# A graph network's planner for five engines gives way to an order written out step by step

## The chip, the cores and the metric

The kernel runs on one core of one Trainium2 chip. A core has five engines that each work through a queue of their own in order: TensorE (PE, matrix products into PSUM banks; PEld is its loading of weights), VectorE (DVE), ScalarE (ACT), GpSimd (POOL) and SyncE (SP), which here only issues DMAs. Engines wait for one another through semaphores. The metric is the device time of one execution in microseconds; smaller is better.

## The reference

Thirty-two graphs ("frames") of 512 nodes with 256 features pass through four attention layers, all with the same 512 x 512 adjacency. After each layer comes x = layernorm(x + layer(x)).

```python
# layer 0: 8 heads of 32, then a two-layer MLP
scores = q k^T / sqrt(32);  attn = softmax(where(adj > 0, scores, -1e9))
x1 = LN(x + attn v) * g1 + b1
y  = LN(x1 + relu(x1 w1 + bias1) w2 + bias2) * g2 + b2
# layer 1: e = leaky_relu(s1[n] + s2[m], 0.2), masked softmax, times h = x W
# layer 2: e = leaky_relu((x W1)(x W2)^T, 0.2), masked softmax, times x W3, relu
# layer 3: as layer 1 with 4 heads of 64, then elu
```

All of it is in float32.

## The kernel before

`fast_path` holds the frames' computation. It doesn't issue instructions as it goes; it describes each frame as steps (`Op`), with the engine, an assumed time in ns, the function that issues the instructions, and the buffers read and written. `Plan.__call__` finds from the buffers which step needs which. A frame has 74 steps on PE, 95 on DVE, and fewer than 130 on each other engine; 32 frames and the preparation of weights and mask make 2391 steps on PE, 3087 on DVE, 3911 on ACT, 884 on POOL and 245 on SP. `plan.place` then puts the steps in order in a model of the engines, `plan.emit` issues them in that order, and the engines' queues get exactly this order. About six frames are in flight at once.

What sets the order: `graph(0)` is placed alone first, which gives each step its place in tenths of a frame (`when`). `due` turns that into a due time: `PACE` 81.87 us per frame, plus a table of where each tenth should stand (`TENTHS`, with other tables for the first four and the last five frames). At each point `place` takes, among the steps that can start soonest, the one that is due first. `safe` refuses a step that could leave no buffer for an earlier frame. A step that needs a buffer gets the one of its kind that, in the model, came free first. Buffers are shared by all frames: 8 PSUM banks, 8 "p" (128 x 4 x 512, attention weights), 9 "t", 7 "y", 6 "x", 4 "e", 3 "v" and some small ones.

Steps of a frame that the prediction names, by the line that issues them:

- L1376 on SP loads x. L932 (`transposed`) transposes 128 x 128 blocks on PE; L1047 does so for the heads' outputs, L1015 for the softmax sums (`sums_back`).
- L749 (`product`) is every full-width product: projections, the MLP, layers 1 and 2. It can be issued as whole 128*128 products, or cut into four with 32 columns of weights each (128*32); `emit` chooses, with the assumed costs of a change of form in `CHANGE`.
- Layer 0, per group g of four heads and block m of 128 nodes: L1064 (`exps`) forms four heads' scores with 32 rows each (32*128) in four banks; ACT takes exp of them (L1068) into a p; DVE multiplies p by the mask (L1116); L1123 multiplies by v (128*32). For the softmax sums, the p's are added up by DMAs that POOL issues (L1002, `add_dma`), then halves are folded, then SP copies one half (L1142), and L1095 sums over the partitions. The last frame sums on PE alone.
- Layer 1: L749 makes v; `gates` sends one column through ACT, a transpose (L1212), a DMA to DRAM (L1216) and a DMA that broadcasts it to all partitions (L1222); DVE makes four blocks of p (L1241) and masks them (L1244); L749 multiplies p by v.
- Layer 2: L749 makes scores, ACT and DVE the masked exponentials, L749 the output.
- Layer 3: as layer 1, with four heads; DVE L1320 (four) and L1327 make a p, L1335 multiplies by q (128*32), L1311 sums.
- `normalise` (L973 to L983): statistics on DVE, the root on ACT, the scaling on ACT.

The array's forms matter to the text below: a matmul record of form 32*128 or 128*32 is one of four that run side by side. An f32 product shows as two records.

Of the kernel before, what the change touches and what calls it, by code (L numbers as in the profile page):

```python
# [9 lines left out]
FP = mybir.dt.float32  # L10
# [19 lines left out]
WAYS = 6  # L30
PACE = 81.87
STAY = 0.00
START = (0, 10.17, 59.24, 97.18, 85.64)
EARLY = 186.52

TENTHS = (0, 35.72, 65.32, 68.92, 152.58, 202.32, 246.27, 266.73, 356.34, 362.66, 490.49)
FIRST = (
    (0, 35.72, 65.32, 62.35, 138.44, 202.98, 246.27, 266.73, 356.34, 362.66, 490.49),
    (-28.44, 35.72, 73.98, 55.02, 197, 202.32, 246.27, 266.73, 356.34, 362.66, 490.49),
    (-31.13, 30.72, 65.32, 68.92, 152.58, 202.32, 246.27, 266.73, 356.34, 362.66, 490.49),  # L40
    (0, 35.77, 65.37, 68.97, 152.63, 202.32, 246.27, 266.73, 356.34, 362.66, 490.49),)
LAST = (
    (0, 35.72, 65.32, 68.92, 152.58, 202.32, 246.27, 266.73, 354.73, 363.36, 490.49),
    (0, 35.72, 65.32, 68.92, 152.58, 202.32, 246.27, 266.73, 356.34, 362.66, 490.49),
    (0, 35.72, 65.32, 68.92, 152.58, 202.26, 246.21, 266.73, 356.34, 412.91, 557.81),
    (-0.21, 35.51, 65.11, 68.71, 152.37, 202.11, 226.96, 232.14, 316.44, 341.17, 500.04),
    (-6.23, 29.49, 59.09, 8.93, 61.49, 76.67, 155.18, 191.54, 257.43, 316.36, 394.47),)
# [391 lines left out]
SIGNAL = 70  # L439
SWITCH = 100  # L440
CHANGE = {0: 196, 1: 213, 2: 126}


class Slot:
# [3 lines left out]
    def __init__(self, kind):  # L448
        self.kind, self.index, self.users, self.ends, self.graph = kind, None if kind else 0, 0, 0.0, None
        self.first = self.last = None  # L450


class Op:
    def __init__(self, engine, ns, run, graph, rank, port, lag, tiling, ways):
        self.engine, self.ns, self.run, self.graph, self.rank = engine, ns, run, graph, rank
        self.port, self.lag, self.tiling, self.ways = port, lag, tiling, ways
        self.then, self.missing, self.slots, self.ready = [], 0, [], 0.0


class Plan:  # L460
# [10 lines left out]
    def clear(self):  # L471
        self.ops, self.graph, self.rank, self.start = [], 0, 0, 0.0
        self.log = {}

    def begin(self, graph, start=0.0):


        self.graph, self.rank, self.start = graph, 0, start

    def __call__(self, engine, ns, run, reads=(), writes=(), port=False, lag=0, tiling=0, ways=None):  # L480
        op = Op(engine, ns, run, self.graph, self.rank, port, lag, tiling, ways or {tiling: 0})
        if not op.rank:
            op.ready = self.start
        self.rank += 1
        needs = {}
        for is_write, group in ((False, reads), (True, writes)):
            for item in group:
                slot, part = (item[0], item[1:]) if isinstance(item, tuple) else (item, None)
                if slot not in op.slots:
                    op.slots.append(slot)  # L490
                    slot.users += 1
                    if slot.first is None:
                        slot.first = op.rank
                    slot.last = op.rank
# [19 lines left out]
    def profile(self, graph):  # L514

        ops = [op for op in self.ops if op.graph == graph]
        live = {kind: [0] * len(ops) for kind in self.counts}
        for slot in {id(s): s for op in ops for s in op.slots if s.kind}.values():
            for r in range(slot.first, slot.last + 1):
                live[slot.kind][r] += 1  # L520
        return live

    def place(self, urgency, ways, stay=0.0, early=1e12,):
# [3 lines left out]
        held_by = {g: self.profile(g) for g in {op.graph for op in self.ops}}  # L527
        engines = {e: 0.0 for e in (PE, DVE, ACT, POOL, SP, DMA)}
        waiting = {e: [] for e in engines}
        free = {k: [(0.0, i) for i in range(n)] for k, n in self.counts.items()}  # L530
        todo, held = {}, {}
        for op in self.ops:
            todo.setdefault(op.graph, set()).add(op.rank)
            if not op.missing:
                waiting[op.engine].append(op)
        order, front, ended = sorted(todo), {g: 0 for g in todo}, {}
        port, port_by, end, tiling = 0.0, None, 0.0, 0
        self.trace = []

        def safe(op, kind, new):  # L540
            spare = len(free[kind]) - len(new)
            if spare < 0:
                return False
            have = spare
            for g in order:
                mine = held.get((g, kind), [])
                have += len(mine)
                if g == op.graph:
                    have += len(new)
                    mine = mine + new  # L550
                r, rows = front[g], held_by[g][kind]
                ahead = sorted(s.first for s in mine if s.first > r)
                for i, stop in enumerate(ahead + [len(rows)]):
                    if stop > r and max(rows[r:stop]) + len(ahead) - i > have:
                        return False
                    r = max(r, stop)
                if g == op.graph:
                    return True

        while todo:  # L560
            choice = None
            for e, ops in waiting.items():
                found = []
                for op in ops:
                    if order[0] + ways <= op.graph:
                        continue
                    due = urgency(op)
                    t = max(engines[e], op.ready, ended.get(op.graph - ways, 0.0))
                    if op.graph >= 0:
                        t = max(t, due - early)  # L570
                    if op.port and port_by is not e:
                        t = max(t, port)
                    if choice and t > choice[0]:
                        continue
                    wants = {}
                    for s in op.slots:
                        if s.index is None:
                            wants.setdefault(s.kind, []).append(s)
                    if all(safe(op, kind, new) for kind, new in wants.items()):
                        for kind, new in wants.items():  # L580
                            t = max(t, sorted(free[kind])[len(new) - 1][0])
                        if op.tiling != tiling and e is PE:
                            due += stay
                        found.append((t, due, op))
                if found:
                    best = min(found, key=lambda f: f[:2])
                    if choice is None or best[0] < choice[0]:
                        choice = best
            assert choice, "no instruction can be placed: too few buffers"
            t, _, op = choice  # L590
            if op.engine is PE and op.tiling != tiling:
                t, tiling = max(t, engines[PE] + SWITCH), op.tiling
            waiting[op.engine].remove(op)
            for s in op.slots:
                if s.index is None:
                    pick = min(free[s.kind])
                    free[s.kind].remove(pick)
                    s.index, s.graph = pick[1], op.graph
                    held.setdefault((op.graph, s.kind), []).append(s)
            engines[op.engine] = t + op.ns  # L600
            if op.port:
                port, port_by = t + op.ns, op.engine
            done = t + op.ns + op.lag + SIGNAL
            end = max(end, done)
            for s in op.slots:
                s.users -= 1
                s.ends = max(s.ends, done)
                if not s.users and s.kind:
                    free[s.kind].append((s.ends, s.index))
                    held[s.graph, s.kind].remove(s)  # L610
            for other in op.then:
                other.missing -= 1
                other.ready = max(other.ready, done if other.engine != op.engine or op.lag
                                  else t + op.ns)
                if not other.missing:
                    waiting[other.engine].append(other)
            left = todo[op.graph]
            left.remove(op.rank)
            while front[op.graph] not in left and left:
                front[op.graph] += 1  # L620
            ended[op.graph] = max(ended.get(op.graph, 0.0), t + op.ns + SIGNAL)
            if not left:
                del todo[op.graph]
                order.remove(op.graph)
# [842 lines left out]
```

## Time and profile before

| | us |
|---|---|
| median of 3 runs | 2871.28 (2866.46 to 2874.03) |
| the profiled execution | 2871.61 |
| its span, first to last instruction | 2869.7 |
| first product starts, last ends (from the span's start) | 7.7, 2852.4 |

Most of the span is periodic: TensorE repeats one order every 86 us, for example from 606.3 to 692.3 us. Busy shares in such a frame are about 100% for TensorE, 88% for VectorE, 68% for ScalarE, 31% for GpSimd; the DMA engines are busy 73% of the time.

| line, what | count | mean us of one |
|---|---|---|
| L1116 DVE mask of a p, layer 0 | 256 | 2.464 |
| L1327 DVE mask of a p, layer 3 | 128 | 2.423 |
| L1068 ACT exp of a bank | 1024 | 0.599 |
| L1002 POOL issue of an adding DMA | 372 | 0.873 |
| L990 POOL addition 128 x 512 | 192 of the form y<-y,x | 1.441 |

A profile's busy time is the sum of records. On ACT and DVE the next instruction starts before the record of the last one ends: the exps of L1068 follow each other at 0.477 us, the masks of L1116 at 2.20 us from start to start. On PE the records' ends are modelled, so times from start to start are used below.

The four parts of a frame's adding DMAs move 10 MB per frame, and they make up most of the DMA traffic: 325 of 425 MB.

### The profile page before, as it was taken

What the parts mean: (1) busy time and instruction counts of PE and PEld (TensorE: products, weight loads), DVE (VectorE), ACT (ScalarE), POOL (GpSimd) and SP (SyncE); (2) the same over time, 40 slices, a digit from 0 to 9 for tenths busy, and PEclk for the clock granted to TensorE, in tenths of its full rate; (3) what the DMA queues carried; (4) which work ended last, traced back from release to release, by engine and by line L of the source; (5) the groups of instructions that cost most, each with busy time, mean ns of one, the idle gap of its engine ahead of it and who ended that gap; (6) DMA issues with size and microseconds to landing.
All of it is one profiled execution on the core that took longest, in us unless ns stands there. A gap on an engine that the chain in (4) does not pass through costs nothing.

```text
span 2869.7 us, 49717 instructions
## 1 busy us (share of the span) xinstructions
PE 2802.0 (98%) x19058; PEld 1507.2 (53%) x19058; DVE 2436.6 (85%) x4076; ACT 1884.6 (66%) x4104; POOL 871.5 (30%) x962
## 2 busy tenths in 40 slices
PE   8889999999999999999999999999999999999996
PEld 3345455555555555555555555555555555554562
DVE  5467888988888988888888888998888998889877
ACT  4566667666676666676666676666676766677553
POOL 1223333323333223333323333323333323333312
PEclk9899999999999999999999999999999999999998
DMA  7855777777776777777777777777777777775115
GB/s 168 169 115 122 159 159 151 156 156 149 164 162 151 155 157 149 162 166 149 155 156 149 162 165 154 149 156 148 163 165 157 148 159 149 160 165 114 41 51 139
DMA packets 101188, 425.07 MB, mean 148 GB/s; under 512 B 10256, under 2 KB 46224, under 8 KB 59152
## 3 DMA queue, kind: packets, MB, share of 16 engines
q0 software_dynamic: 49600, 325.08, 57.6%
q1 hardware_dynamic: 51344, 96.75, 11.7%
q8 instruction: 152, 2.49, 0.3%
q14 instruction: 92, 0.75, 0.1%
HBM read 63.38 MB, written 17.10 MB: 28 GB/s over the span
## 4 chain that ended last, share of the span: by engine, by line
PE 87%; DVE 7%; DMA 2%; ACT 2%; issue 2%; POOL 0%; SPq 0%; DVEq 0%; ACTq 0%; POOLq 0%
PE bank L749 54%; PE bank L1064 8%; PE bank L1123 8%; PE bank L1335 7%; PE bank L932 4%; DVE p L1116 3%; PE bank L1047 2%; PE bank L1311 1%; PE bank L1095 1%; PE bank L1015 1%; DVE p L1320 1%; DMA x<-in_x_dram 1%; ACT p L1068 1%; DVE st L973 1%; DMA p<-p 0%
## 5 line engine op out<-in xcount | busy, mean ns | idle before, releaser
L1002 POOL DMA_DIRECT2D p<-p x372 | 323.3, 873 | 1766.4 <-DMA p<-p 587.7
L1116 DVE TENSOR_TENSOR p<-p,edge_t 128x2048 f32<-128x2048 f32 x256 | 628.5, 2464 | 61.4 <-ACT p L1068 61.2
L920 ACT ACTIVATE t<-bank 128x512 f32<-128x512 f32 x640 | 373.1, 595 | 393.6 <-PE bank L1123 129.9
L1068 ACT ACTIVATE p<-bank 128x512 f32<-128x512 f32 x1024 | 537.4, 599 | 81.9 <-PE bank L1064 81.5
L749 PE MATMUL bank<-v,p 128*128 128x257 f32 (+1 forms) x2912 | 468.0, 384 | 4.3 <-DVE p L1244 3.8
L749 PEld LDWEIGHTS bank<-v,p 128*128 128x128 f32 (+1 forms) x2912 | 367.7, 159 | 90.7 <-issue 26.6
L973 DVE BATCH_NORM_STATS2 st<-y 128x6 f32<-128x256 f32 x768 | 316.1, 412 | 36.2 <-POOL y L990 26.6
L1320 DVE TENSOR_SCALAR p<-p,e,e 128x512 f32<-128x512 f32 x512 | 333.1, 684 | 0.4 <-DMA p<-row 0.3
L990 POOL TENSOR_TENSOR y<-y,x 128x512 f32<-128x512 f32 x192 | 275.3, 1441 | 156.7 <-ACT y L1295 98.4
L1327 DVE TENSOR_TENSOR p<-p,edge_t 128x2048 f32<-128x2048 f32 x128 | 310.2, 2423 | 2.2
L1064 PE MATMUL bank<-t,t 32*128 32x512 f32 x2048 | 300.7, 646 | 0.0
L983 ACT ACTIVATE x<-y,rs,rs 128x256 f32<-128x256 f32 x512 | 277.7, 596 | 18.0 <-DVE rs L980 15.1
L1123 PE MATMUL bank<-p,v 128*32 128x512 f32 x2048 | 274.0, 607 | 15.2 <-DVE p L1116 11.4
L1335 PE MATMUL bank<-p,v 128*32 128x512 f32 x2048 | 241.5, 597 | 3.7 <-DVE p L1327 3.2
L749 PE MATMUL bank<-t,wqkv 128*32 128x512 f32 (+1 forms) x944 | 243.8, 596 | 0.9 <-ACT t L920 0.9
L920 ACT ACTIVATE v<-bank 128x264 f32<-128x264 f32 (+2 forms) x384 | 176.1, 459 | 80.0 <-PE bank L749 77.0
L749 PE MATMUL bank<-t,t 128*128 128x512 f32 (+1 forms) x656 | 225.2, 592 | 0.0
L1064 PEld LDWEIGHTS bank<-t,t 32*128 32x128 f32 x2048 | 84.1, 185 | 173.4 <-issue 86.4
L932 PE MATMUL bank<-ident,x 128*128 128x128 f32 x1024 | 149.6, 280 | 14.2 <-DMA x<-in_x_dram 10.3
L974 DVE BATCH_NORM_AGGREGATE mv<-st 128x2 f32<-128x6 f32 x768 | 139.9, 182 | 26.3
L932 PEld LDWEIGHTS bank<-ident,x 128*128 128x128 f32 x1024 | 118.2, 142 | 78.8 <-issue 37.7
L749 PEld LDWEIGHTS bank<-t,t 128*128 128x128 f32 (+1 forms) x656 | 94.3, 167 | 111.2 <-issue 107.2
(119 smaller groups left out, 3855.7 us busy)
## 6 DMA issues: line engine op xcount, KB each, us to landing
p<-p POOLq DMA_DIRECT2D x248, 1024.0 KB, 7.2
p<-p POOLq DMA_DIRECT2D x124, 512.0 KB, 5.8
p<-row SPq DMA_DIRECT2D x32, 1024.0 KB
x<-in_x_dram SPq DMA_DIRECT2D x32, 512.0 KB
out_dram<-x SPq DMA_DIRECT2D x32, 512.0 KB
p<-p SPq DMA_DIRECT2D x31, 512.0 KB
e<-row SPq DMA_DIRECT2D x32, 256.0 KB
t<-in_adj_dram SPq DMA_DIRECT2D x4, 256.0 KB
```

The lines of the kernel that those rows point to most:

```text
L749: nc.tensor.matmul(out[c:c + w, :], left[:, c:c + w], right, start=start, stop=stop)
L920: act(170 + n * 0.84, lambda: nc.scalar.activation(to(T(dst)), frm(T(src)), AF.Copy), [src], writes)
L932: nc.tensor.transpose(T(bank)[:, (2 * k + c) * P:(2 * k + c + 1) * P], T(src)[:, c0 + c, k * P:(k + 1) * P], ident)
L973: nc.vector.bn_stats(T(st)[:, c, :], T(y)[:, c, :])
L1002: nc.gpsimd.dma_start(a, b, accum_op=ALU.add)
L1064: nc.tensor.matmul(T(banks[j]), T(kT)[r, g, m * P:(m + 1) * P], T(qT)[r, g, :], start=True, stop=True)
L1068: act(600, lambda j=j: nc.scalar.activation(T(p)[:, j, :], T(banks[j]), AF.Exp, scale=1.0 / math.sqrt(D0)), [banks[j]], [(p, j)])
L1116: dve(2420, lambda p=p, m=m: nc.vector.tensor_tensor(T(p), T(p), T(edge_t)[:, m, :].unsqueeze(1).to_broadcast([P, J, N]), ALU.mult), [p, ( ...
L1123: nc.tensor.matmul(T(av)[j * D0:(j + 1) * D0, :], T(v)[:, m, h * D0:(h + 1) * D0], T(p)[:, j, :], start=(m == 0), stop=(m == NC - 1))
L1320: nc.vector.tensor_scalar(T(p)[:, 2 * m + i, :], T(G)[:, h, :], T(e1)[:, r:r + 1], T(e02)[:, r:r + 1], ALU.mult, ALU.max)
L1327: nc.vector.tensor_tensor(p4, p4, T(edge_t)[:, m0:m0 + 2, :].unsqueeze(2).to_broadcast([P, 2, 2, N]), ALU.mult)
L1335: nc.tensor.matmul(T(av)[w:w + 32, :], T(q)[:, m0 + m, 2 * H3 + k * P + w:2 * H3 + k * P + w + 32], T(p)[:, 2 * m + w // D3, :], start=(m0 ...
```

## The change

`place`, `profile`, the due times (`PACE`, `TENTHS`, `FIRST`, `LAST`, `START`, `EARLY`) and the placeholder steps (`skip`) are taken out. In their place stands ORDER: for each engine a string. A letter stands for a frame (A to Z, a to f; "." for the preparation) and means "the next step of this frame on this engine that hasn't been issued"; a number ahead of it skips so many of those. `follow` walks the five strings with a model of the engines, and hands each step that needs a buffer the one that came free first in that model. The model's times are new. `ways` chooses the form of `product` along the whole PE string.

```diff
+GRAPHS = ".ABCDEFGHIJKLMNOPQRSTUVWXYZabcdef"
+ORDER = {
+    "PE": (
+        "1A1.2.A1.1..3A.1A1AAA2.2.1..A2.AB..1AB2AAB2A1BA2AAAB1A2B1B2AAB2AAAB1CA1BC2BB2BCBB1B2B1CCB1CC2BC3B1DB"
...
+    "SP": (
+        "A1.3.2.11.2.8.1.3.1.5.B.9.5..6.D1.2.2.2.2.C1..FEABAACBBAADCCBBEAGDDCCFBHEEDDGCIFFEEHDJGGFFEIKHHGGFJL"
...
-SIGNAL = 70
-SWITCH = 100
-CHANGE = {0: 196, 1: 213, 2: 126}
+SIGNAL = 40
+SWITCH = 92
+ENTRY = {1: 121, 2: 34}
+TAIL = {PE: 160, DVE: 85, ACT: 120, POOL: 130, SP: 0, DMA: 0}
+IDLE, SPAN, SLOW = 1500, 2000, 1700
...
-    def place(self, urgency, ways, stay=0.0, early=1e12,):
...
+    def ways(self, order):
...
+        costs, steps = {0: 0.0, 1: 1e15, 2: 1e15}, []
+        for op in order:
+            came, new = {}, dict.fromkeys(costs, 1e15)
+            for way, extra in op.ways.items():
+                cost = {w: c + (SWITCH + op.enter(way) if w != way else 0) for w, c in costs.items()}
+                came[way] = min(cost, key=cost.get)
+                new[way] = cost[came[way]] + extra
+            costs = new
+            steps.append(came)
...
+    def follow(self, order):
...
+        for e, steps in order.items():
+            queues[e], at = [], 0
+            for step in steps:
+                if step.isdigit():
+                    at = 10 * at + int(step)
+                else:
+                    queues[e].append(left[e, GRAPHS.index(step) - 1].pop(at))
+                    at = 0
+        self.ways(queues[PE])
...
+            for s in op.slots:
+                if s.index is None:
+                    s.index = free[s.kind].pop(0)[1]
...
-        plan.place(urgency, WAYS, 1e3 * STAY, 1e3 * EARLY)
+        plan.follow(ORDER)
         plan.emit(tiling)
```

The assumed times of most steps change too; they are used by the model alone. Examples:

```diff
-        plan(PE, 970, run, [(kT, g), (qT, g)], banks, tiling=1)
+        plan(PE, 858, run, [(kT, g), (qT, g)], banks, tiling=1)
...
-            act(600, lambda j=j: nc.scalar.activation(
+            act(482, lambda j=j: nc.scalar.activation(
...
-                dve(2420, lambda p=p, m=m: nc.vector.tensor_tensor(
+                dve(2205, lambda p=p, m=m: nc.vector.tensor_tensor(
...
-        plan(POOL, 950, run, reads, [dst, started])
-        plan(DMA, 5600 if src else 2650, None, reads + [started], [dst], lag=2500)
+        plan(POOL, 850, run, reads, [dst, started], lag=300)
+        plan(DMA, 5000 if src else 2500, None, reads + [started], [dst], lag=1300 if src else 1900)
```

The instructions that a step issues are the same as before. The changed file also holds some text twice (the classes, the general path's layer functions and the head of `fast_path`); the later definitions replace the earlier ones.

## The prediction

> **What bounds the kernel now.** I read the page first, then the waits of TensorE in three stretches, the busy time by stretch, and the timeline of TensorE in one steady frame.
>
> The page, parts 1 and 2:
>
> ```profile
> PE 2802.0 (98%) x19058; PEld 1507.2 (53%) x19058; DVE 2436.6 (85%) x4076; ACT 1884.6 (66%) x4104; POOL 871.5 (30%) x962
> PEclk9899999999999999999999999999999999999998
> ```
>
> TensorE is busy all the way. Its records are drawn out, so 98% doesn't say that nothing is to be had; it says that time has to come out of its queue. What it waits for, between 344 and 2580 us (all of it), and then before 344 us (the longest):
>
> ```profile
> PE bank L1123 <- DVE p L1116: 2.1, 8, 0.6
> PE bank L1335 <- ACT x L983: 0.3, 1, 0.3
> PE bank L1015 <- ACT e L920: 0.2, 1, 0.2
> ...
> PE bank L932 <- DMA x<-in_x_dram: 10.3, 2, 7.7
> PE bank L1123 <- DVE p L1116: 9.3, 5, 2.7
> PE bank L749 <- DVE p L1244: 3.8, 1, 3.8
> ```
>
> In 2236 us of steady state it waits 2.6 us. So no faster VectorE or ScalarE helps there, and a new order helps only if TensorE's own queue gets shorter. At the start, and at the end, it does wait (columns: stretch, its length, busy time of PE, PEld, DVE, ACT and POOL, granted clock, DMA share, GB/s):
>
> ```profile
> 0.00:90.00 90.00, 76.10 (x560) 32.20 (x564) 48.62 (x83) 46.94 (x90) 11.19 (x26) 0.94 0.78 174
> 90.00:180.00 90.00, 73.83 (x541) 32.55 (x537) 44.49 (x69) 48.29 (x101) 30.47 (x29) 0.87 0.71 140
> 606.00:692.00 86.00, 85.84 (x578) 46.77 (x574) 76.08 (x125) 58.55 (x129) 26.53 (x31) 1.00 0.73 157
> 2770.00:2870.00 100.00, 74.60 (x430) 38.56 (x428) 74.47 (x146) 44.90 (x99) 23.39 (x22) 0.92 0.45 107
> ```
>
> Now the timeline of TensorE in that steady frame. The three forms are 128*128 (whole array), 32*128 (scores of layer 0, four row groups side by side) and 128*32 (four column groups):
>
> ```profile
> 613.31 7.03 PE L749 MATMUL bank<-t,t 128*128 128x512 f32 x16
> 620.18 1.88 PE L749 MATMUL bank<-t,wqkv 128*128 128x512 f32 x4
> 643.17 1.03 PE L1047 MATMUL bank<-ident,t 128*128 128x128 f32 x8
> 644.14 1.92 PE L1335 MATMUL bank<-p,v 128*32 128x512 f32 x16
> 645.99 1.14 PE L1064 MATMUL bank<-t,t 32*128 32x512 f32 x8
> 647.06 0.66 PE L932 MATMUL bank<-ident,x 128*128 128x128 f32 x4
> 647.55 0.27 PE L1212 MATMUL bank<-ident,gs 128*4 128x128 f32 x1
> ```
>
> From start to start, sixteen records with 512 columns take 6.87 us, 0.429 each; two transposes (8 records) at 0.109 each should take 0.874. But L1047 to L1335 is 0.97: about 0.092 more, at a change of form. The scores (8 records, four abreast: 0.858) take 1.07: 0.121 on entry and 0.092 to the next form. L1335 takes 1.85 against 4 x 0.429: 0.034 on entry. L932 takes 0.49 against 0.437: 0.056; other 128*128 products after a change pay 0.104. A change of form thus costs 0.213 us into 32*128, 0.126 into 128*32, 0.148 (transposes) or 0.196 into 128*128. Such a frame changes form 26 times in 86.0 us.
>
> **What the Trainium skill says.** "TensorEngine Tiling (Array Packing)", Key Properties: changing the tiling mode, not just the tile, drains TensorE. The trace agrees: 0.088 to 0.093 us extra in the middle of every kind of change. "TensorE: Matmul & The Clock Gate", What's actually happening: after an idle window of about 3.4 us the clock falls to half, and returns after a busy one. The trace agrees in kind: half-clock stretches of 3.4 or 6.8 us stand at 58, 68, 96, 106, 113 and 174 us, and before most of them is a gap of only 2.3 to 3.8 us. "DMA: Bandwidth & Descriptors", Queues, rings and completion order: each DMA engine takes turns between its queues, packet by packet. In the trace the broadcast of layer 1's row to all partitions waits among the adding DMAs: from issue to the first step that uses it 3.6 to 5.8 us in steady state, 8.4 at the start.
>
> **The change part by part.** (1) Removed: `place`, `profile`, the due times, `skip`. Added: `follow`, which reads ORDER. All this runs while the program is built and costs the chip nothing. Read off, the strings use up every step: 2391 of PE, 3087 DVE, 3911 ACT, 884 POOL, 245 SP, as before. No instruction is added or removed, apart from how `product` is cut.
>
> (2) PE's order. I read the string against the steps of `graph` and let `ways` take the cheaper form where two are allowed. It has 730 changes of form. The records of the trace before have 837. By kind, before to after: into 32*128 254 to 247, into 128*32 326 to 261, into transposes 164 to 165, into other 128*128 93 to 57. Priced: 7 x 0.213 = 1.5; 65 x 0.126 = 8.2; 36 x 0.196 = 7.1, less 0.1. Products cut in four cost 0.026 more, 255 of them before and 244 after: 0.3. Sum 16.9 us, nearly all on the path.
>
> Does this bookkeeping hold? A frame's steps at steady pace sum to 81.7 us; the 31 like frames 2532.6, the last 93.9 (its sums are products, not DMAs), preparation 7.8: 2634.3. Changes add 137.7 and the cut 6.6: 2778.6. The first product starts at 7.7, the last ends 17.2 before the end. 7.7 + 2778.6 + 17.2 = 2803.5, so 66 of 2869.7 are left over: waits and half clock. Set against the trace by each frame's L1212, 42 arise before 227 us, 3 between there and 2634, 21 after. So the steady part is explained to 0.15%.
>
> (3) The start. In the order before, 0.9 us of products stood between the third scores of group 1 and the product that wants their p, in frames A and B. ScalarE needs 4 x 0.48 and VectorE 2.2 for it: hence gaps of 2.67 at 56 and 94 us. Now 4.3 and 6.1 us stand there; where 1.7 stood before B's first, 3.5. x of the fourth frame was issued at 92.2, behind the copy at L1142 that SP waited for, and TensorE waited 2.6 for it at 110; now that load is in the first twenty on SP, ahead of the copy. Gaps of 10 us go, and half-clock stretches of 23.8 us with them, half of it lost time: 22. But A's sums (L1095) arrive through a chain of adding DMAs that landed at 103.8, and TensorE already waited 1.3 there. A quicker TensorE waits there longer; I let the sums come 5 us sooner, not 16, since the DMA share is 0.78. After it the x wait and its slow stretch go (2.6 + 3.4), less 2 for a new slow stretch. Net 9; bounds 0 and 18. SP also moves the load of wqkv from first to thirteenth: 3.4 MB up to and with it, which the packets of the trace reached at 15 us; TensorE wants it at about 14. That is a loss of 1 to 3, within these bounds.
>
> (4) The steady part. Some distances in PE's queue shrink. From L1212 of layer 1 to its product stood 15.3 us in every frame; now 11.3 to 18.2, mean 13.8. The chain is 1.9 for the row, 3.6 to 5.8 for the broadcast, 4.04 for VectorE's five steps (6.25 to 6.7 in most frames, with others between them; 7 to 8.6 measured before), 0.3 for signals: 9.8 to 14.6. Behind a late product, all PE steps stand in line, and ScalarE's evacuations behind them. The sums of layer 0 had 8 to 11 us to spare; their distance falls from 41.7 to 33.7 at worst: just enough. Elsewhere 0.4 us stands where 1.3 did (L1015 to L1047). Zero at best; 0.6 us a frame, 15, at worst. I take 5. Buffers were, and are, taken in the order in which the planner thinks they come free; only its times differ, so numbers move and a wait for a late reader could come: within the same bounds.
>
> (5) DVE, ACT and POOL steps move by 2 to 3 places on average. Their cover is that TensorE didn't wait for them: VectorE has 10 us free in 86, ScalarE 27. In the last frames the order hardly differs; I take 2 of the 21, bounds 0 and 6.
>
> Sum: 16.9 + 9 + 2 - 5 = 23 us off 2869.7, a span of 2847; 1.9 lies around the span in that execution (2871.61), and it stands at the median shown (2871.28). Forecast 2848 us.
>
> **The rivals.** First, more: if the start falls to the 15 us that first loads and a cold array take, and the end to 15, then 16.9 + 27 + 6 = 50 us go: 2821. For it: the waits at the start are short leads. Against it: the DMA chain at 104.
>
> Second, no change: the queue is shorter, but stalls grow by 26 us, 1.1 us a frame in 24 frames: about 2869. For it: shortened distances and the spread of DMA times. Against it: most frames keep more than the chain needs.
>
> Third, slower: the broadcast at L1222 lands late among the adding DMAs, and the product of layer 1 waits. A wait of 1.5 us that brings a half-clock stretch costs 1.5 + 1.7. In 16 of 24 frames that is 51, less the 26 gained: 2896. It decides from 35 us of new loss, 1.5 us a frame. For it: in frames with 11.3 to 12.7 us a broadcast of 5.6 is already late by up to 1.5. Against it: those are 6 or 7 frames, and a late TensorE lets the next chains catch up.
>
> That the change does nothing is excluded by the count of forms.
>
> **How the numbers follow.** Forecast (2832 to 2862) 0.72; more than that 0.08; no change 0.10; slower 0.10. 0.3%, 8.6 us, is about what a measurement can tell from no change. So faster 0.80, same 0.10, slower 0.10. The range 2830 to 2865 takes the bounds of (3) to (5) at their likelier ends.
>
> **What would show it.** Changes of form in the records of the changed kernel: 730. Time between layer 1's L1212 of the fifth and the 26th frame: 8 us less than 1812 if nothing stalls. Gaps at 56 and 94 us gone, the wait at L1095 longer, no wait for x at 110 us. I am wrong if TensorE waits more than 15 us between 344 and 2580, or if the start gives nothing.

## The result and the profile after

| | median us | lowest to highest |
|---|---|---|
| before (4 runs; the first 3 are those above) | 2869.11 | 2866.46 to 2874.03 |
| after | 2947.23 | 2937.41 to 2952.62 |
| ratio | 1.0266 | 1.0235 to 1.0298 (95%) |

The change costs 2.7%. The profiled execution took 2948.04 us with a span of 2946.3. First the page of the kernel after, parts 1 and 2:

```profile
PE 2815.8 (96%) x18938; PEld 1527.1 (52%) x18938; DVE 2317.1 (79%) x4076; ACT 1857.6 (63%) x4104; POOL 946.6 (32%) x962
PEclk9999999999999999999999999999999999999998
```

VectorE and ScalarE are less busy than before, in a longer span: the time that was added isn't work of theirs. The waits of TensorE between 344 and 2650 us (releaser, sum, times, longest), the four largest:

```profile
PE bank L1585 <- DVE p L2077: 13.8, 7, 6.2
PE bank L1958 <- DVE p L1951: 11.9, 13, 1.7
PE bank L1931 <- DMA p<-p: 11.7, 6, 3.8
PE bank L1958 <- DVE y L2090: 8.2, 2, 7.8
```

L1585 is `product` (L749 before), L1951 and L1958 are layer 0's mask and product (L1116, L1123), L1931 its sums (L1095), L2077 layer 1's mask (L1244), L2074 and L2153 the first steps of VectorE that read a broadcast row (L1241, L1320), L2049 and L2055 the row's store and broadcast (L1216, L1222). All waits of this view add up to 72 us; before they were 2.6. Between 344 and 2650 us there are also ten stretches of half clock, 44 us together, so 22 us of lost work; before had none there. The stretches (columns as before):

```profile
0.00:90.00 90.00, 75.24 (x540) 33.36 (x540) 46.64 (x83) 44.70 (x88) 10.02 (x24) 1.00 0.79 186
90.00:180.00 90.00, 82.10 (x793) 35.84 (x788) 55.59 (x93) 52.25 (x111) 31.02 (x31) 0.94 0.73 145
606.00:692.00 86.00, 86.00 (x544) 46.89 (x544) 70.72 (x113) 55.69 (x124) 32.82 (x28) 1.00 0.71 147
1700.00:1786.00 86.00, 79.85 (x498) 44.26 (x497) 63.00 (x111) 51.21 (x115) 27.36 (x29) 0.96 0.69 149
2846.00:2946.00 100.00, 76.96 (x437) 39.91 (x435) 75.75 (x152) 46.72 (x103) 22.58 (x24) 0.91 0.44 106
```

The start is better (full clock in the first 90 us, 82 busy in the second 90, where 74 was). Some steady stretches are full, others have lost 6 us. To place the loss, each step of TensorE's string was matched with its records, and its start was set against the queue priced as in the prediction. Start minus priced start, in us, at layer 1's gate transposition (L2045; before L1212) of some frames, counted from 0:

| frame | 1 | 5 | 10 | 15 | 20 | 25 | 29 |
|---|---|---|---|---|---|---|---|
| before | 50.0 | 51.3 | 51.6 | 51.7 | 52.9 | 53.3 | 53.2 |
| after | 36.9 | 40.2 | 67.0 | 88.1 | 110.6 | 128.1 | 143.4 |

So 13 us are won in the first two frames, as hoped, and 103 lost in the 24 from frame 5 to frame 29, in jumps (places where the difference grows from one step to the next). The timeline around one of them, the kernel after, all engines:

```profile
1722.54 1.75 POOL L1838 DMA_DIRECT2D p<-p  x2 [0.88 <-DMA p<-p]
...
1724.20 0.27 SPq L2049 DMA_DIRECT2D row<-gT  x1
...
1729.05 0.34 SPq L2055 DMA_DIRECT2D e<-row  x1
...
1738.12 1.92 DVE L2074 TENSOR_SCALAR p<-e,e,e 128x512 f32<-128x512 f32 x4 [6.68 <-DMA e<-row]
...
1740.07 2.29 DVE L2077 TENSOR_TENSOR p<-p,edge_t 128x2048 f32<-128x2048 f32 x1
1742.28 2.29 DVE L1951 TENSOR_TENSOR p<-p,edge_t 128x2048 f32<-128x2048 f32 x1
1742.62 3.77 PE L1585 MATMUL bank<-v,p 128*128 128x257 f32 x8 [6.15 <-DVE p L2077]
```

Two adding DMAs are issued from 1722.5 on, and the small store of the row at 1724.2 stands among them: its broadcast can be issued only 4.85 us later. The broadcast takes 9.1 more. VectorE, which works in order, stands for 6.68 us at the first step that reads it, and TensorE for 6.15 behind VectorE. At such a gap the clock falls to half (6.8 us from 1741). In VectorE's own waits between 344 and 2650 us, before and then after:

```profile
DVE p L1241 <- DMA e<-row: 18.7, 14, 2.2
```

```profile
DVE p L2074 <- DMA e<-row: 37.1, 13, 6.7
DVE p L2153 <- DMA p<-row: 14.6, 5, 7.5
```

Why is the row later? From the store's issue to that of its broadcast, in layer 1, the mean was 1.43 us before and is 2.92 after (1.68 and 2.64 in layer 3). In the 1.2 us after a store's issue, packets of 4 KB or more kept the 16 DMA engines busy for 8% of the time before and for 58% after. Where this share was under 30%, the store took 1.46 us before (49 of 53 stores) and 1.43 after (20 of 52); where it was over 90%, 3.8 us after (26 stores; before there was one). The old, periodic order put nearly every store into a quiet moment between adding DMAs; the new order doesn't repeat from frame to frame and puts half of them into a busy one. This fits the Trainium skill, "DMA: Bandwidth & Descriptors", Queues, rings and completion order: each engine takes turns between queues by packets.

Layer 1's broadcast itself didn't get slower: by its semaphore it landed 4.3 us after its issue before and 4.1 after (means). Layer 3's did, from 5.0 to 6.8.

For every jump of over 0.5 us between 344 and 2650 us (97 us together, about the 72 of waits and the 22 of half clock), the chain of latest releasers was followed back, through the queues, to the first stop that has no busy engine behind it. This places the loss; it doesn't prove a cause:

| the chain ends at | us |
|---|---|
| VectorE waiting for a row (L2074 28.2, L2153 17.9) | 46 |
| TensorE waiting for layer 0's added sums (L1931) | 15 |
| GpSimd waiting for an adding DMA before the next | 8 |
| a p or another buffer held by a transfer | 7 |
| a loop TensorE, ScalarE or VectorE, TensorE without a transfer | 21 |

### The profile page after: what moved, and what is told of

It is laid out like the page before. It is cut to its first block, busy times and chain, and to the rows that moved or that the text cites. A ratio compares the mean times of both kernels' runs of the same rounds, so it can differ in the third digit from the quotient of the medians.

```text
span 2946.3 us, 49510 instructions
## 1 busy us (share of the span) xinstructions
PE 2815.8 (96%) x18938; PEld 1527.1 (52%) x18938; DVE 2317.1 (79%) x4076; ACT 1857.6 (63%) x4104; POOL 946.6 (32%) x962
## 5 line engine op out<-in xcount | busy, mean ns | idle before, releaser
L1951 DVE TENSOR_TENSOR p<-p,edge_t 128x2048 f32<-128x2048 f32 x256 | 618.0, 2418 | 93.6 <-ACT p L1904 93.0
L1904 ACT ACTIVATE p<-bank 128x512 f32<-128x512 f32 x1024 | 566.1, 600 | 146.4 <-PE bank L1900 126.3
L1585 PE MATMUL bank<-v,p 128*128 128x257 f32 (+1 forms) x2672 | 474.9, 383 | 17.2 <-DVE p L2077 13.8
L1585 PEld LDWEIGHTS bank<-v,p 128*128 128x128 f32 (+1 forms) x2672 | 371.6, 166 | 112.9 <-issue 40.9
L1826 POOL TENSOR_TENSOR y<-y,x 128x512 f32<-128x512 f32 x192 | 292.1, 1539 | 350.0 <-ACT y L2128 210.3
L2153 DVE TENSOR_SCALAR p<-p,e,e 128x512 f32<-128x512 f32 x512 | 292.1, 597 | 21.9 <-DMA p<-row 16.0
L2160 DVE TENSOR_TENSOR p<-p,edge_t 128x2048 f32<-128x2048 f32 x128 | 296.4, 2318 | 1.2
L1958 PE MATMUL bank<-p,v 128*32 128x512 f32 x2048 | 267.4, 604 | 25.7 <-DVE p L1951 16.7
L2168 PE MATMUL bank<-p,v 128*32 128x512 f32 x2048 | 246.9, 604 | 10.2 <-DVE p L2160 5.6
L1585 PE MATMUL bank<-t,wqkv 128*32 128x512 f32 (+1 forms) x1100 | 245.8, 598 | 4.3 <-ACT p L1904 2.5
L1756 ACT ACTIVATE v<-bank 128x258 f32<-128x258 f32 (+2 forms) x384 | 169.6, 456 | 96.2 <-PE bank L1585 92.3
L1585 PE MATMUL bank<-t,t 128*128 128x512 f32 (+1 forms) x644 | 227.4, 592 | 0.0
L1819 ACT ACTIVATE y<-y,rs,rs 128x256 f32<-128x256 f32 x256 | 144.2, 598 | 32.1 <-DVE rs L1816 31.8
```

The source lines that it names most:

```text
L1585: nc.tensor.matmul(out[c:c + w, :], left[:, c:c + w], right, start=start, stop=stop)
L1756: act(55 + n * 0.83, lambda: nc.scalar.activation(to(T(dst)), frm(T(src)), AF.Copy), [src], writes)
L1819: act(492, lambda c=c: nc.scalar.activation(T(dst)[:, c, :], T(y)[:, c, :], AF.Identity, bias=T(nm)[:, c:c + 1], scale=T(rs)[:, c:c + 1]), ...
L1826: pool(1235, lambda: nc.gpsimd.tensor_tensor(T(dst)[:, w, :], T(a)[:, w, :], T(b)[:, w, :] if row is None else T(row).unsqueeze(1).to_broa ...
L1904: act(482, lambda j=j: nc.scalar.activation(T(p)[:, j, :], T(banks[j]), AF.Exp, scale=1.0 / math.sqrt(D0)), [banks[j]], [(p, j)])
L1951: dve(2205, lambda p=p, m=m: nc.vector.tensor_tensor(T(p), T(p), T(edge_t)[:, m, :].unsqueeze(1).to_broadcast([P, J, N]), ALU.mult), [p, ( ...
```

## The experiments

Theory A: landing times; the new order reaches steps that wait for a transfer before it lands. Theory B: no slack between the engines, with or without transfers. Theory C: the buffers that `follow` gives out tie steps together. All runs have medians of 4 executions or more, against the kernel before on the same chip (2868 to 2872).

**Order or planner.** The new file with the former order of all five engines in its strings:

```diff
     "PE": (
-        "1A1.2.A1.1..3A.1A1AAA2.2.1..A2.AB..1AB2AAB2A1BA2AAAB1A2B1B2AAB2AAAB1CA1BC2BB2BCBB1B2B1CCB1CC2BC3B1DB"
+        "AA....A..AAAAA....2.A..1ABBA1ABA1ABA1ABA1ABABBAA1AABA1BB1BCBC1BCB1BCB1BCBCCBCB1BBCBAAAA1CDDDCDDAADAA"
...
```

> The new planner (its way of giving out buffers, of choosing forms and of reading an order), but every engine follows the order of the kernel before. Theory A (adding DMAs: in the new order VectorE, and TensorE behind it, reaches steps that wait for a transfer before it lands) and theory B (the new order leaves no slack between steps of TensorE, ScalarE and VectorE, with or without transfers) both put the loss into the order: 2869, within 12 us. Theory C (buffers given out by their free time tie steps together that were free before): 2920 or more, with waits of TensorE of 40 us or more between 344 and 2580 us.

Measured 2867.21, ratio 0.9992 (0.9985 to 0.9999). TensorE's waits between 344 and 2580 us are one line:

```profile
PE bank L1937 <- DVE p L1930: 1.5, 7, 0.4
```

L1937 and L1930 are layer 0's product and mask; line numbers shift from run to run. Theory C is out in its general form: with the old order, planner, buffers and `ways` cost nothing, so the loss comes with the order. What the new order loses through the buffers that go with it, this run doesn't show; the chains above put at most 7 us there.

**Small adding DMAs**, in the new and in the old kernel (main line of the edit):

```diff
-            nc.gpsimd.dma_start(a, b, accum_op=ALU.add)
+            nc.gpsimd.dma_start(a[:, 0:1], b[:, 0:1], accum_op=ALU.add)
```

> The new order, every adding DMA cut to a quarter of its columns (three quarters of the sums are left out; the edges of layers 0, 1 and 3 count as all ones and the sums are taken four times, so that numbers stay finite). Theory A: of the 97 us that TensorE loses in jumps over 0.5 us between 344 and 2650 us, 76 go back along the chain of releasers to a step that waits for a transfer; so 2947 - 76 = 2871, taken as 2845 to 2890, and the small store ahead of the row's broadcast takes 1.2 to 1.5 us, where it took 2.9 and 2.6 on the mean. Theory B: 2925 or more. Theory C: 2925 or more.

> The kernel before with the same small adding DMAs (the same part left out). TensorE waited 2.6 us in its whole steady state, so there is nothing there to be won: all theories 2850 to 2870, less than the 2869 only by what the start and the end waited for sums. If it gains more than 25 us, the adding DMAs cost time in a way that the waits don't show, and the second run says less about the order.

The whole programs took 11852 and 11836 us, since values out of range sent them on through the general path; the fast path ahead of it is in the traces in full. Its last product ended at 2860.0 us, where it was 2934.1: 74 us less, against 76 expected. With the old order it ended at 2837.0, where it was 2852.4: 15 less. The two orders, 82 us apart, are 23 apart without the large transfers. The store of layer 1's row took 1.65 us on the mean (2.92 with whole DMAs), a little above the 1.2 to 1.5 expected. VectorE's waits at the rows, new order, small DMAs:

```profile
DVE p L2077 <- DMA e<-row: 5.7, 6, 1.8
DVE p L2156 <- DMA p<-row: 2.9, 2, 2.5
```

So most of the loss hangs on the adding DMAs. Through which wait, this doesn't say.

**Which wait.** The new order with all DMAs whole; the broadcast reads a fixed row that is written once (e5), the sums read a constant (e6), both (e7). The flag that calls the general path is put out of reach in all three (main lines of the edits):

```diff
-            to(), T(row)[:R, :].rearrange("r q -> (r q)").partition_broadcast(P)),
-            [row], [G, started])
+            to(), fixed[:R, :].rearrange("r q -> (r q)").partition_broadcast(P)),
+            [], [G, started])
...
-                nc.tensor.matmul(T(sm)[j * 32:(j + 1) * 32, :], pick[:, g, :], T(p)[:, j, :],
+                nc.tensor.matmul(T(sm)[j * 32:(j + 1) * 32, :], pick[:, g, :],
+                                 ones.unsqueeze(1).to_broadcast([P, NC, P]) if g == 2 else T(p)[:, j, :],
...
-            plan(PE, 871, lambda: sums(2, low, True, True), [low], [sm], tiling=2)
+            plan(PE, 871, lambda: sums(2, low, True, True), [], [sm], tiling=2)
```

> The new order with all adding DMAs whole, but the broadcast of layers 1 and 3 reads a fixed row of DRAM instead of the stored gates, so that it no longer waits for the small store to land (the gates of the sources are left out; the store itself still runs). Theory A1 (the late broadcast stops VectorE at the first step of layer 1 or 3, and the masks queued behind it come late to TensorE): about 46 of the 97 us of jumps go back to these two steps, so 2947 - 46 = 2901, between 2885 and 2915. Theory A2 (the sums of layer 0 that TensorE waits for itself): 2930 or more. Theory A3 (adding DMAs give the p buffers back late): 2930 or more.

> The new order, but TensorE's last product of layer 0's sums reads a constant instead of the added sums, so that it waits for no adding DMA (the sums of layer 0 are left out; all DMAs still run). Theory A1: only the 15 to 23 us that go back to this product: 2924 to 2934. Theory A2: 2895 or less. Theory A3: 2930 or more.

> Both edits together. Theory A1 with the sums as a second, smaller cause: 2947 - 46 - 15 to 23 = 2878 to 2890. Theory A3: above 2920, as the adding DMAs still hold their buffers as long as before. If it comes near 2873, the small adding DMAs' gain of 74 us is all explained by these two waits.

| | us | ratio to before | against after |
|---|---|---|---|
| e5, row early | 2914.84 | 1.0156 (1.0129 to 1.0182) | -32 |
| e6, sums early | 2939.38 | 1.0231 (1.0207 to 1.0256) | -8 |
| e7, both | 2892.37 | 1.0089 (1.0066 to 1.0111) | -55 |

The row is the largest single cause: 32 us, where the chains had put 46. The sums alone give 8, which isn't clear of noise (e6's interval overlaps that of after); with the row out of the way they give 22 more (e7 against e5), which is. That both together give more than 40 may be because with one gone the other still stops the same stretch of queue; with runs of one kernel 12 to 17 us apart the surplus isn't firm. e6 and e7 came out 5 and 2 us above what was expected. VectorE still waits for the broadcast of the fixed row in e7, but 7.6 us where it was 52, and TensorE still waits too:

```profile
DVE p L2077 <- DMA e<-fixed: 5.0, 7, 1.5
DVE p L2156 <- DMA p<-fixed: 2.6, 2, 1.5
```

```profile
PE bank L1961 <- DVE p L1954: 11.7, 15, 2.3
PE bank L1587 <- DVE p L2080: 5.8, 3, 3.8
PE bank L2171 <- DVE p L2163: 4.8, 3, 2.5
```

These are the products of layers 0, 1 and 3 behind their masks. Followed back as above, 39 of the 56 us of jumps left in e7 are loops without a transfer. So theory B seems to hold for a rest that the rows had hidden; no edit takes that rest away by itself.

**How near to the edge.** The store of the row made twice, one after the other, in the old and the new order; the broadcast reads the second copy (not shown):

```diff
+        def twice():
+            nc.sync.dma_start(T(row)[:R, :], T(gT)[:R, :])
+            nc.sync.dma_start(T(row)[R:2 * R, :], T(row)[:R, :])
```

> The old order in the new planner, with the small store ahead of the broadcast made twice, one after the other, so that the row lands 1.2 to 3 us later in each of 64 places (nothing is left out). Theory A (slack decides): TensorE stands behind masks that have room there, 2869 to 2885. Theory B: likewise. If it costs over 40 us, the old order is as near to the edge as the new one, and the slack is not what sets the two apart.

> The new order with the same double store. Theory A1 (the row's landing is on TensorE's path): 2947 + 30 to 60 = 2977 to 3007, three times or more what the old order pays. Theory B (the loss stands in the steps between the engines, the row is an accident): under 2960.

In layer 1, store to broadcast became 4.50 us in the old order (3.1 more) and 5.66 in the new (2.7 more). The old order went to 2907.67 (40 more than e1), the new to 3119.19 (172 more than after, far above the 2977 to 3007 expected). VectorE's waits at the rows, first the old order, then the new:

```profile
DVE p L2057 <- DMA e<-row: 82.8, 26, 8.2
DVE p L2136 <- DMA p<-row: 1.4, 1, 1.4
```

```profile
DVE p L2078 <- DMA e<-row: 101.3, 21, 9.3
DVE p L2157 <- DMA p<-row: 47.3, 12, 9.3
```

In the old order VectorE waits 70 us more (84 where e1 has 14), and 40 us of that become time: some slack lies between VectorE and TensorE, less than expected (2885 at most), and the bound set ahead, 40, is just reached. In the new order 97 us more of waiting (149 where after has 52) become 172: little can lie between, and other losses come on top. Stretches of half clock alone grow from 44 us to 147 between 344 and 2650 us. Layer 3's row, to which the old order gives 12 us from the broadcast's issue, is on the path only in the new one.

**Orders.** Only ORDER differs from here on. e4 takes the new order up to 340 us of the planner's own time and the old one for the rest. e8, e9 and e12 to e15 come from a search by small moves of single steps, against different costs (the expectations say which); their times on the chip are what counts here.

> The new planner and, on every engine, the new order up to 340 us of the planner's own time, then the order before for all steps that are left. The new order's first five frames were 13 us ahead in the trace (loss against the priced queue 36.9 us at frame 1 where it was 50.0), the old order loses 3 us in 2300 us of steady state. Theories A and B: 2869 - 14 = 2855, between 2845 and 2866. Theory C: over 2900.

> Nothing but ORDER differs from the new kernel. The order was found by small moves of single steps, starting from the order of the run before (new start, old rest), against costs in which the small store lands up to 4.5 us late when an adding DMA is in flight, durations of VectorE, ScalarE and GpSimd vary by up to 5 to 7 per cent, and VectorE and GpSimd don't exclude each other. TensorE's queue has 676 changes of form, 54 fewer than the new order. Theory A (the new order was fitted to landing times that the chip doesn't keep): 2830, between 2805 and 2855, faster than both kernels. Theory B (a TensorE queue with so few changes of form always stands too close to VectorE and ScalarE): 2880 or more.

> The twin of the run above: the same start, the same kind and length of search, but against the planner's own costs, in which a store lands after 1.1 us whatever else moves and nothing varies. 684 changes of form. Theory A: it repeats the new order's fault, 2925 to 2990, and the store ahead of the broadcast takes 2.2 us or more on the mean. Theory B: about as slow as the run above, within 20 us. If both are faster than 2860, the fault lies in the particular order of the change and not in the costs it was fitted to.

> Nothing but ORDER differs from the new kernel. The same search as for the run e8 that missed (small moves from the order with the new start and the old rest, late stores, varied durations), but the costs now also let VectorE's mask and scaling steps and GpSimd's adds shut each other out, fully or in part, as the traces of before and after show it (a mask step 2281 ns alone, 3209 ns where an add had begun). 665 changes of form. Theory A with the shared port as the part that e8 lacked: 2835, between 2810 and 2858, faster than both kernels. Theory B (so few changes of form leave too little room between TensorE, ScalarE and VectorE): 2880 or more.

> The same costs and length of search, but started from the new order itself instead of the spliced one, 681 changes of form at the end. If the cost of landing and sharing was all that the new order lacked, its own repair by small moves also ends at 2810 to 2865; if the interleaving of frames that it chose is at fault beyond that, 2890 or more.

> Nothing but ORDER differs from the new kernel. The order of e13 searched on, with wider spread in the costs (durations of VectorE, ScalarE and GpSimd up to 10 per cent longer at random, stores up to 5 us late), 653 changes of form. If slack against late transfers and shut-out steps is what turns a cheap TensorE queue into time, 2830 to 2858, below e13 (2866) and the spliced order (2863). If the spread adds nothing that the chip asks for, 2860 or more.

> The same search, from e12's order: 620 changes of form, the fewest of all orders here. If the number of changes decides once slack is in the costs, this is the fastest, 2825 to 2855. If the slack that the chip needs isn't in the costs, it falls behind e14 by 10 us or more.

| order | changes of form | us | ratio to before | jumps over 0.5 us, 344 to 2650 |
|---|---|---|---|---|
| before (e1) | 837 | 2867.21 | 0.9992 (0.9985 to 0.9999) | 2 |
| after | 730 | 2947.23 | 1.0266 (1.0235 to 1.0298) | 97 |
| e4 | 830 | 2862.61 | 0.9957 (0.9941 to 0.9974) | 2 |
| e8 | 676 | 2983.68 | 1.0405 (1.0380 to 1.0431) | 120 |
| e9 | 684 | 2956.53 | 1.0305 (1.0283 to 1.0326) | 100 |
| e12 | 654 | 2882.47 | 1.0044 (1.0030 to 1.0057) | 57 |
| e13 | 671 | 2865.77 | 0.9989 (0.9980 to 0.9997) | 37 |
| e14 | 653 | 2833.22 | 0.9869 (0.9853 to 0.9884) | 23 |
| e15 | 620 | 2822.13 | 0.9827 (0.9813 to 0.9841) | 12 |

(The changes of e12 and e13 are those counted when their orders are read; their expectations said 665 and 681.)

e9, searched against the planner's own costs, repeats the fault at the time forecast: VectorE waits 48 us at the rows. e8 is a plain miss: 2984 where 2830 was expected. Its costs knew late stores, and VectorE's waits at the rows fell to 10 us; but they let VectorE and GpSimd run side by side. They don't, and TensorE's largest waits in e8 are for masks of layers 0 and 3 (24 and 16 us). GpSimd's additions in e8, from the groups of its instructions:

```profile
L1829 POOL TENSOR_TENSOR y<-y,x 128x512 f32<-128x512 f32 x192 | 318.1, 1668 | 394.1 <-ACT y L2131 203.1 <-ACT y L2197 96.1 <-DVE y L1889 77.7
```

1.668 us of one, where before had 1.441. With the exclusion in the costs, e12 takes 101 us less at fewer changes of form; still it missed, above the 2858 expected, on the side of theory B. e13, which repairs the new order itself by small moves, takes 81 us less than after and lies just above its range (2865). With a wider spread on top, and searched on from there, e14 comes in as forecast and e15 3 us below its range; the order with the fewest changes is the fastest. So few changes of form do no harm as such. That room against late and shut-out steps makes the difference is what these runs speak for; each is one order, and none separates the wider spread from the longer search. TensorE's waits in e15 between 344 and 2650 us, the largest two of seven, and VectorE's at the rows:

```profile
PE bank L1965 <- DVE p L1958: 2.0, 3, 0.9
PE bank L1592 <- ACT t L1763: 1.4, 3, 0.7
```

```profile
DVE p L2160 <- DMA p<-row: 4.7, 4, 2.1
DVE p L2081 <- DMA e<-row: 2.7, 1, 2.7
```

In e15 the stores still fall among adding DMAs (51% of the engines' time in the 1.2 us after them; 2.07 us to the broadcast in layer 1). What changed is the room: after the landing of layer 1's broadcast, 2.7 us pass on the mean before VectorE's first step reads it, where after leaves 0.6 and before 0.2. (Before has its room further on: from that step to the mask's end 7.9 us pass, 6.1 in after and 4.8 in e15; without a break it takes 4.2.) e15 beats both kernels, the one before by 1.7% and the one after by 4.2%. e4 gains 7.6 us, at the near end of its range: spliced, the sums of the first frames come later, and TensorE waits 8.1 us for them in three places.

## Why the prediction was wrong

- **Bound and bookkeeping: right.** The 730 changes of form are in the records after. The parts add up: 16.9 (queue) and 13.1 (start) less, 2.0 more to frame 5, 101.3 from there to frame 29 beyond what before lost, 3.4 at the end: 76.7, and the spans differ by 76.6. The queue's saving was there; the steady part lost six times as much.
- **(1) The planner costs nothing: right** (e1; its buffers cost nothing in the old order).
- **(3) Start, 9 forecast: 13.** The x wait of TensorE is one of 5.0 where two of together 10.3 were, the wait for masks 4.9 where 9.3 was, and one stretch of half clock of 10.2 us is left of 34. The wait for added sums, which was to eat much of this, hardly grew (1.7 us where 1.3 was). The load of wqkv cost 1.0, forecast 1 to 3. A new wait of 4.4 us at the transposition of the adjacency (L1654, in the preparation) wasn't foreseen. So the size lies within the bounds given, near by two errors of opposite sign and so partly by luck.
- **(4) The steady part, 5 forecast with 0 to 15: 103. This is the step that failed**, in three ways. First, the chain's duration ("1.9 for the row, 3.6 to 5.8 for the broadcast") was read from a trace in which the stores fell into quiet moments, and taken over into an order in which they don't: store to broadcast is 1.5 us longer in layer 1 and 1.0 in layer 3. The term that was too small is the row: from the gate's transposition to the broadcast's issue 2.4 us on the mean before (1.9 and signals), 3.9 after and up to 6.2; the broadcast kept its time. Second, only the chain's own consumer was charged, the product of layer 1. That wait (L1585 for L2077) is 13.8 us. What VectorE had queued behind the late step came late as well: TensorE waits 11.9 us for layer 0's masks (L1951) and 8.2 for layer 1's outputs (L2090), though not all of that goes back to rows, and half clock takes 22 more. Third, layer 3's row was given no term at all, and the sums of layer 0 were called sufficient ("just enough"); the chains put 18 and 15 us there.
- **(5) "DVE, ACT and POOL steps move by 2 to 3 places on average. Their cover is that TensorE didn't wait for them": wrong.** That cover belonged to the old order. In the new one, by the chains, loops without transfers cost 21 us, and about 40 once the rows are out of the way (e7). The end, 2 less forecast, is 3 more.
- **The rivals.** The third came nearest, the row late among the adding DMAs, with 2896 and a chance of 0.10; but it is the small store that got slower, not layer 1's broadcast. Its point of decision, 35 us of new loss, was passed almost three times over. Its place was too narrow, and what was held against it ("a late TensorE lets the next chains catch up") didn't carry: the jumps go on to the last steady frame.
- **Signs named ahead.** From the fifth to the 26th frame's gate 8 us less than 1812 were due if nothing stalled; it is 1890. The gaps at 56 and 94 us and the wait for x at 110 are gone. "TensorE waits more than 15 us between 344 and 2580" is the sign of being wrong that came true: 72 us.

Why such an order was written isn't known. e9 makes one reason likely: a search against costs that land every store after the same time gives this result again.

## What to carry to other kernels

A transfer's duration in a trace holds for the traffic that was beside it; if an order changes, ask of each small transfer what will be in flight when it is issued. On an engine that works in order, a late operand costs everything queued behind the waiting step, so price the queue, not the consumer. Where an order is fitted to a model, ask which effects the model leaves out: the same kind of search lost 3% against fixed durations (e9), 4% with late stores and spread but without the exclusion of VectorE and GpSimd (e8), about nothing with both (e12, e13), and won 1.7% with a wider spread and a longer search (e15).

## What the hardware showed unexpectedly

From the issue of a store of 2 or 8 KB to that of the DMA that waits for it, 1.4 us passed in a quiet moment and 3.8 among large packets (after). A double store, 3 us more of latency in a chain, cost 40 us in one order and 172 in another.

VectorE and GpSimd shut each other out. A mask step took 2281 ns before where no addition of GpSimd overlapped it (190 of 256) and 3209 where one had begun ahead of it (47); in after 2285 and 2831. GpSimd's additions took 1.27 us at the 25th percentile and over 3.1 at the 95th in after (1.65 before). VectorE's steps that read one operand from a PSUM bank were not slowed: L1886 took 687 ns alone and 684 beside an addition. The Trainium skill, "SBUF — State Buffer", Terms, calls the shared port pair of the two a lock held for the full instruction, whose loser fully blocks. The trace agrees closely. Of the 33 additions that began under a mask in before, 26 ended 1.12 to 1.47 us after it, while an undisturbed one takes 1.27: nearly all of their work came after the mask. In the other 7 the addition won: it took 1.5 to 1.6 us, and the mask, 2.28 us alone, ended 2.16 after it.
